# Graph layer 1 by lists: a 128-wide column selection, a DMA-shifted comparison, four sums in a bank, and half of the placings on ScalarE

## The chip, the cores and the metric

The kernel runs on one core of a Trainium2 chip. The metric is device time in microseconds; three runs of the kernel before gave 1370.18, 1371.73 and 1374.76, the median being 1371.73. The engines are TensorE (PE, with its weight loads PEld), VectorE (DVE), ScalarE (ACT), GpSimd (POOL) and SyncE (SP, which here only issues DMAs). A profile of one execution is read for where the time goes.

## The reference

Four graph layers act in turn on x (2708 x 128) with one sparse matrix adj (2708 x 2708). Each normalises its input, applies relu and adds its result to x. The change touches layer 1 only:

```python
s = node_feats @ msg_w[:, :D].T
d = node_feats @ msg_w[:, D:].T
messages = gelu(s[:, None, :] + d[None, :, :] + msg_b)
aggregated = einsum('ijd,ij->id', messages, adj)
combined = concatenate([node_feats, aggregated], axis=-1)
new_feats = combined @ upd_w.T + upd_b
h = gelu(new_feats) + node_feats            # then a layer norm over h
```

A message exists for every pair (i, j), but it counts only where adj[i, j] is not zero, which are few entries in a row. The diagonal is one of them.

## The kernel before

Rows are taken in 22 tiles (`NT`) of 128, columns in 22 blocks (`NB`) of 124 (`JB`). Layer 0 streams adj once, writes its transpose to memory on SP's queue, and keeps for every row and block the eight largest entries and their columns (`val`, `col`, `S` = 8), the diagonal (`own`) apart. If a row has more, or a tile more than 128 entries in a block, a dense version runs instead; it does not here.

Layer 1 packs the entries of one tile and one block into 128 slots (`E`), so that the gelu runs on slots and not on pairs. For tile t:

- `count_rows` counts the entries of each row and block; `rank` turns the counts into running sums by a matmul with a triangle of ones (`ends`: exclusive and inclusive sums).
- `describe` writes the values, split in three bf16 parts, the columns and the ranks into `xb`.
- `select_rows` makes the 0/1 matrix `sel` [row, slot, block] that says which row fills which slot: one comparison with the exclusive sums, one with the inclusive ones (`later`), and their difference, 128 x 2816 elements each.
- `fetch` multiplies each block's `sel` with `xb`, in two halves of 11 blocks; every slot then has its row's entries and rank (`y`, `lead`).
- `place` picks in each slot its own entry (`value`) and column (`where`), and makes two 0/1 matrices: `selT` [slot, column, block], the column selection, and `mine` [slot, row, block].
- `put_values` multiplies `mine` with `value` on GpSimd, in two halves of 11 blocks (`put`, the placings).
- `turn_columns` transposes `selT` block by block on TensorE, eight to a PSUM bank, and ScalarE copies them out as `cols`.
- `combine` adds, in PSUM, the row's part (`sel` against the three parts `s3` of s) and the column's part (`cols` against `d3`): six matmuls a block, four blocks to a bank. `activate` is the gelu on ScalarE. `gather` multiplies the gelus with `put` and sums all blocks of a tile in a bank, `agg`. `close_tile` adds the diagonal's term (`gs`, the gelu of the own row, times `dg`, a diagonal of `own`) and VectorE copies the sum to `aggT`.
- `sources` prepares s and the own row's gelu for two tiles; `update` does the second half of the layer for four tiles, in eight steps, two of which fall into most tiles.

The order of the work is written by hand in `period(t)` and kept as written on each engine; the semaphores are set from the buffers. A period has six stages k, each with four blocks (two in the last). While tile t is combined, tile t+1 is turned and placed, tile t+2 fetched and placed, tile t+3 ranked and selected. Pools set when a buffer is free: `once` has one buffer (`mine`, `later`, `picked`), `putpool` three halves of `put`, `selpool` four of `sel`, `acc` one bank for `agg`. Three periods run as a fill between the first steps of the layer; period 0 begins near 320 us, the last combine ends near 797 us.

Of the kernel before, what the change touches and what calls it, by code (L numbers as in the profile page):

```python
# [30 lines left out]
P = 128  # L31
# [29 lines left out]
def listed_layers(ctx: ExitStack, tc: tile.TileContext, x, adj, w, out, flag):  # L61
# [186 lines left out]
    with (  # L248
# [2 lines left out]
        tc.tile_pool(name="l1w", bufs=1) as once,  # L251
        tc.tile_pool(name="l1s", bufs=4) as selpool,
        tc.tile_pool(name="l1b", bufs=3) as three,
        tc.tile_pool(name="l1q", bufs=3) as putpool,
        tc.tile_pool(name="l1y", bufs=2, space=PSUM) as ypool,
        tc.tile_pool(name="l1m", bufs=2, space=PSUM) as mpool,
        tc.tile_pool(name="l1p", bufs=1, space=PSUM) as acc,
# [14 lines left out]
        nc.vector.tensor_copy(counts, count.unsqueeze(2).to_broadcast([P, P, NB]))  # L272
        part = fix.tile([P, 1], F32, name="part")
        nc.gpsimd.iota(part, [[0, 1]], base=0, channel_multiplier=1, allow_small_or_imprecise_dtypes=True)
        before = fix.tile([P, 2, P], BF16, name="before")
        nc.vector.tensor_scalar(before[:, 0, :], count, part, None, ALU.is_gt)
        nc.vector.tensor_scalar(before[:, 1, :], count, part, None, ALU.is_ge)
        ident_h = fix.tile([P, P], BF16, name="ident_h")
        nc.vector.tensor_copy(ident_h, ident)
        rows_n = fix.tile([P, NT, NB], BF16, name="rows_n")  # L280
        ends = fix.tile([P, NT, 2, NB], BF16, name="ends")
        d3 = fix.tile([P, NB, 3, D], BF16, name="d3")
        xb = [fix.tile([P, NB, C], BF16, name=f"xb{q}") for q in range(2)]
        for q in range(2):
# [10 lines left out]

        def count_rows(t):
            some = work.tile([P, NB, S], BF16, name="some")
            nc.gpsimd.tensor_scalar(some, val[:, t, :, :], 0.0, None, ALU.is_gt)
            with nc.allow_low_precision("counts up to 8"):
                nc.vector.reduce_sum(rows_n[:, t, :], some, AX.X)  # L300

        def rank(t):
            p = rpool.tile([P, CH], F32, tag="r", name="p_r")
            for q in range(2):
                nc.tensor.matmul(p[:, q * NB : (q + 1) * NB], before[:, q, :], rows_n[:, t, :], start=True, stop=True)
            nc.vector.tensor_copy(ends[:, t, :, :], p[:, 0 : 2 * NB].rearrange("p (q b) -> p q b", q=2))  # L306

        def describe(t):
            x = xb[t % 2]
            rest = work.tile([P, NB, S], F32, name="v_r")  # L310
            split([x[:, :, q * S : (q + 1) * S] for q in range(3)], val[:, t, :, :], rest)
            nc.gpsimd.tensor_copy(x[:, :, 3 * S : 4 * S], col[:, t, :, :])
            nc.gpsimd.tensor_copy(x[:, :, 4 * S], ends[:, t, 0, :])

        def select_rows(t):

            sel = selpool.tile([P, E, NB], BF16, name="sel")
            later = once.tile([P, E, NB], BF16, name="later")
            for q, dst in enumerate((sel, later)):
                nc.vector.tensor_tensor(  # L320
                    dst, counts, ends[:, t, q, :].unsqueeze(1).to_broadcast([P, E, NB]), ALU.is_ge
                )
            nc.vector.tensor_tensor(sel, sel, later, ALU.subtract)  # L323
            state[t] = dict(sel=sel, ys=[])

        def fetch(t, half):

# [12 lines left out]
        def place(t):  # L340

            st = state[t]
            lead = st["lead"]
            slot = work.tile([P, NB], F32, name="slot")
            nc.vector.tensor_scalar(slot, lead[:, 0, :], part, -1.0, ALU.subtract, ALU.mult)
            hot = work.tile([P, NB, S], F32, name="hot")
            nc.vector.tensor_tensor(
                hot,
                count[:, 0:S].unsqueeze(1).to_broadcast([P, NB, S]),
                slot.unsqueeze(2).to_broadcast([P, NB, S]),  # L350
                ALU.is_equal,
            )
            picked = once.tile([P, NB, 4, S], F32, name="picked")
            for half, y in enumerate(st.pop("ys")):
                bs = slice(half * HB, (half + 1) * HB)
                nc.vector.tensor_tensor(
                    picked[:, bs, :, :],
                    y[:, :, 0 : 4 * S].rearrange("p b (q s) -> p b q s", s=S),
                    hot[:, bs, :].unsqueeze(2).to_broadcast([P, HB, 4, S]),
                    ALU.mult,  # L360
                )
            value = work.tile([P, NB], F32, name="value")
            where = work.tile([P, NB], BF16, name="where")
            with nc.allow_low_precision("column numbers"):
                nc.vector.tensor_reduce(where, picked[:, :, 3, :], AX.X, ALU.max)
            selT = work.tile([P, JB, NB], BF16, name="selT")
            nc.vector.tensor_tensor(  # L367
                selT, counts[:, 0:JB, :], where.unsqueeze(1).to_broadcast([P, JB, NB]), ALU.is_equal
            )
            nc.vector.reduce_sum(value, picked[:, :, 0:3, :], AX.XY)  # L370
            mine = once.tile([P, P, NB], BF16, name="mine")
            nc.vector.tensor_tensor(  # L372
                mine, counts, lead[:, 1, :].unsqueeze(1).to_broadcast([P, P, NB]), ALU.is_equal
            )
            st["value"], st["selT"], st["mine"] = value, selT, mine

        def put_values(t, half):

            st = state[t]
            put = putpool.tile([P, HB, P], F32, name="put")  # L380
            bs = slice(half * HB, (half + 1) * HB)
            nc.gpsimd.tensor_tensor(  # L382
                put,
                st["mine"].rearrange("p i b -> p b i")[:, bs, :],
                st["value"][:, bs].unsqueeze(2).to_broadcast([P, HB, P]),
                ALU.mult,
            )
            st["put", half] = put

        def turn_columns(t, b0):  # L390

            st = state[t]
            if b0 == 0:
                st["cols"] = work.tile([P, NB, E], BF16, name="cols")
            n = min(8, NB - b0)
            p = ps.tile([P, 8, E], BF16, tag="ps", name="p_c")
            for b in range(n):
                nc.tensor.transpose(p[0:JB, b, :], st["selT"][:, :, b0 + b], ident_h)  # L398
            nc.scalar.copy(st["cols"][0:JB, b0 : b0 + n, :], p[0:JB, 0:n, :])  # L399

        own_rows = {}

        def sources(k):

# [22 lines left out]
            split([s3[:, q, :, :] for q in range(3)], sb[:, :, 0, :], rest)  # L427
            gs = three.tile([P, 2, D], F32, name="gs")
            nc.scalar.activation(gs, sb[:, :, 1, :], AF.Gelu)
            own_rows[k] = s3, gs  # L430

        def combine(t, k):
# [24 lines left out]
        def gather(t, k):  # L457

            st = state[t]
            m = size(t)  # L460
            if k == 0:
                st["agg"] = acc.tile([P, P], F32, name="agg1")
            g = st.pop(("g", k))
            for b in range(4 * k, min(4 * k + 4, NB)):
                put = st["put", b // HB][:, b % HB, 0:m]
                nc.tensor.matmul(st["agg"][:, 0:m], g[:, b - 4 * k, :], put, start=(b == 0), stop=False)  # L466

        aggs = {}

        def close_tile(t):  # L470

            st = state.pop(t)
            m = size(t)
            gs = own_rows[t // 2][1]
            if t // 4 not in aggs:
                aggs[t // 4] = work.tile([D, 4, P], F32, name="aggT")
            nc.tensor.matmul(st["agg"][:, 0:m], gs[0:m, t % 2, :], st["dg"][0:m, 0:m], start=False, stop=True)
            nc.vector.tensor_copy(aggs[t // 4][:, t % 4, 0:m], st["agg"][:, 0:m])


        STEPS = 8
# [51 lines left out]
        def period(t):  # L533

            now, c, b, a = (0 <= t + q < NT for q in range(4))
            last = 0 <= t - 1 < NT
            for k in range(GB):
                if now:
                    combine(t, k)
# [8 lines left out]
                    gather(t, k - 1)  # L548
                if k in (1, 2) and b:
                    fetch(t + 2, k - 1)  # L550
                if k == 1:
                    if c:
                        put_values(t + 1, 0)
                    if a:
                        describe(t + 3)
                if k == 2:
                    if now:
                        dg = work.tile([P, P], F32, name="dg1")
                        nc.scalar.activation(dg, ident, AF.Identity, scale=own[:, t : t + 1])
                        state[t]["dg"] = dg  # L560
                        if t % 2 == 0 and t + 2 < NT:
                            sources(t // 2 + 1)
                    if a:
                        select_rows(t + 3)
                    if now and t + 4 < NT:
                        count_rows(t + 4)
                    updates(t)
                    if c:
                        put_values(t + 1, 1)
                if k >= 3 and c:  # L570
                    turn_columns(t + 1, 8 * (k - 3))
                if k == 3 and b:
                    place(t + 2)


        def enter(g):
# [72 lines left out]
        nc.vector.reduce_sum(flag, lost[:, 0, :], AX.X)  # L649
        over = fix.tile([P, 2], F32, name="over1")  # L650
        many = once.tile([P, NT, NB], BF16, name="many")
        nc.vector.tensor_scalar(many, ends[:, :, 1, :], float(E), None, ALU.is_gt)
        nc.vector.reduce_sum(over[:, 0:1], many, AX.XY)
        nc.vector.tensor_scalar(many, val[:, :, :, S - 1], 0.0, None, ALU.is_gt)
        nc.vector.reduce_sum(over[:, 1:2], many, AX.XY)
# [708 lines left out]
```

## Time and profile before

| what | us |
|---|---|
| median of three runs | 1371.73 |
| the profiled execution | 1372.74 |
| its span | 1370.9 |
| layer 0, fill, loop of layer 1 (from the span's start, near) | 0 to 245, 245 to 320, 320 to 797 |
| layers 2 and 3 | from about 800 |
| mean granted TensorE clock (share of full) | 0.905 |

The profile lists busy time by engine, groups of instructions by line (count, busy time, mean of one, idle time of the engine before them and what ended it), a timeline, and the chain of work that ended last: each piece in it was released by the piece before. A matmul's time is from its start to its modelled end and overlaps the next one; in the chain only the part that counts is shown. A line such as `128*124 128x124` gives the weights' rows and columns and then the operand's shape.

### The profile page before, as it was taken

The page shows a single profiled execution, that of the slowest core. Times are in us where ns is not written, and L with a number is a line of the kernel's source. Part 1 is how long each engine was busy: PE and PEld are TensorE (multiplying, and loading weights), DVE is VectorE, ACT ScalarE, POOL GpSimd, SP SyncE. Part 2 cuts the span into 40 slices and gives each one's busy share as a digit, 9 for nine tenths or more (in the row PEclk, how much of TensorE's full clock was granted, in tenths as well). Part 3 has the DMA queues.
Part 4 walks back from the last instruction along what each step waited for, and adds up shares of the span by engine and source line. Part 5 has one row for each costly group of instructions (what it writes and reads, how often), then busy time and mean ns, then how long its engine had stood idle before and what let it go on. Part 6 is the DMA issues. An engine that isn't in the chain of part 4 may idle for free.

```text
span 1370.9 us, 22846 instructions
## 1 busy us (share of the span) xinstructions
PE 1177.2 (86%) x8590; PEld 945.0 (69%) x8590; DVE 968.1 (71%) x2971; ACT 602.4 (44%) x1188; POOL 374.9 (27%) x303
## 2 busy tenths in 40 slices
PE   4997878248999999999999968898967999999975
PEld 1554445247999999999999943333445898997763
DVE  5999999994677676877799237666554667666551
ACT  4865655134333333343343321222244666765633
POOL 2111120454566465555564320000000001001001
PEclk9999985557999999999999979999987998998985
DMA  9488854000000000000000044444210000000000
GB/s 364 160 305 289 278 200 163 16 0 1 1 1 2 1 1 1 2 1 1 1 2 1 2 141 162 162 163 143 86 29 1 1 1 9 9 1 10 7 1 13
DMA packets 47930, 93.72 MB, mean 68 GB/s; under 512 B 5654, under 2 KB 18022, under 8 KB 45102
## 3 DMA queue, kind: packets, MB, share of 16 engines
q1 hardware_dynamic: 41220, 89.40, 18.7%
q10 hardware_dynamic: 6590, 2.77, 0.8%
q8 instruction: 69, 1.13, 0.4%
q14 instruction: 51, 0.42, 0.1%
HBM read 61.44 MB, written 30.72 MB: 67 GB/s over the span
## 4 chain that ended last, share of the span: by engine, by line
PE 43%; DVE 41%; issue 7%; DMA 4%; POOL 2%; ACT 2%; ACTq 0%; POOLq 0%; DVEq 0%
PE att L853 11%; DVE col L215 9%; DVE val L214 6%; PE agg L466 6%; PE p_m L442 4%; PE p_c L398 4%; PE p_m L446 4%; PE p_agg L742 3%; DVE selT L367 2%; DVE later L320 2%; DVE mask L745 2%; PE y L334 2%; DMA a<-adjT 2%; PE p_o L888 2%; DVE sel L323 2%
## 5 line engine op out<-in xcount | busy, mean ns | idle before, releaser
L853 PE MATMUL att<-hv,wt 128*128 128x129 f32 (+3 forms) x1936 | 241.3, 282 | 5.7 <-DVE att L870 4.8
L853 PEld LDWEIGHTS att<-hv,wt 128*128 128x128 f32 (+3 forms) x1936 | 222.6, 191 | 22.5 <-issue 10.4
L847 DVE SCALAR_TENSOR_TENSOR wt<-e,mask 128x1024 f32<-128x1024 f32 (+2 forms) x132 | 144.8, 1098 | 68.0 <-PE att L853 64.0
L382 POOL TENSOR_TENSOR put<-mine,value 128x1408 f32<-128x1408 bf16 x44 | 156.7, 3562 | 115.0 <-DVE mine L372 64.9
L442 PE MATMUL p_m<-s,sel 128*128 128x128 bf16 x1452 | 179.2, 233 | 2.4 <-ACT s L289 1.2
L843 ACT ACTIVATE e<-row,minus_one,rho 128x1024 f32<-128x1024 f32 (+2 forms) x132 | 149.1, 1141 | 67.3 <-DVE wt L847 65.3
L446 PE MATMUL p_m<-d,cols 124*128 124x128 bf16 (+1 forms) x1452 | 163.6, 221 | 0.0
L118 POOL TENSOR_TENSOR n_r<-n_r,minus_half 128x4 f32<-128x4 f32 (+2 forms) x30 | 34.8, 1161 | 453.0 <-DVE n_r L117 441.2
L442 PEld LDWEIGHTS <-sel 128*128 128x128 bf16 x1452 | 149.9, 161 | 3.8 <-issue 2.9
L466 PE MATMUL agg<-put,g 128*128 128x128 f32 (+1 forms) x968 | 138.2, 284 | 14.6 <-DVE ends L306 12.3
L194 PE MATMUL acc<-a,hs 128*128 128x512 f32 (+2 forms) x264 | 122.3, 598 | 31.9 <-DMA a<-in_adj 21.9
L466 PEld LDWEIGHTS agg<-put,g 128*128 128x128 f32 x968 | 120.2, 194 | 16.3 <-issue 16.2
L398 PE MATMUL p_c<-ident_h,selT 128*124 128x128 bf16 x484 | 123.2, 396 | 1.1 <-ACT cols L399 1.1
L742 PE MATMUL p_agg<-a,hs 128*128 128x512 f32 (+2 forms) x264 | 117.7, 592 | 5.0 <-DMA a<-adjT 5.0
L398 PEld LDWEIGHTS <-selT 128*124 128x124 bf16 x484 | 121.2, 336 | 1.1 <-issue 1.1
L215 DVE FIND_INDEX8 col<-val,a 128x8 uint16<-128x124 f32 (+1 forms) x441 | 117.0, 274 | 0.0
L454 ACT ACTIVATE g<-p_m 128x512 f32<-128x512 f32 x132 | 74.0, 560 | 91.5 <-PE p_m L446 90.7
L399 ACT COPY cols<-p_c 124x1024 bf16<-124x1024 bf16 (+1 forms) x66 | 62.0, 941 | 116.2 <-PE p_c L398 116.2
L446 PEld LDWEIGHTS <-cols 124*128 124x128 bf16 (+1 forms) x1452 | 109.6, 102 | 0.6 <-issue 0.6
L194 PEld LDWEIGHTS acc<-a,hs 128*128 128x128 f32 (+1 forms) x264 | 49.1, 207 | 75.7 <-issue 42.4
L214 DVE MAX8 val<-a 128x8 f32<-128x124 f32 (+1 forms) x441 | 101.0, 264 | 0.0
L223 PEld LDWEIGHTS p_T<-ident,a 128*128 128x128 f32 x484 | 59.6, 147 | 54.9 <-ACT aT L227 25.9
(238 smaller groups left out, 1839.4 us busy)
## 6 DMA issues: line engine op xcount, KB each, us to landing
a<-in_adj SPq DMA_DIRECT2D x21, 1354.0 KB, 7.8
adjT<-aT SPq DMA_DIRECT2D x105, 256.0 KB, 2.6
a<-adjT SPq DMA_DIRECT2D x20, 1280.0 KB, 6.4
adjT<-aT SPq DMA_DIRECT2D x21, 74.0 KB, 2.7
a<-adjT SPq DMA_DIRECT2D x4, 370.0 KB
out<-xs SPq DMA_DIRECT2D x21, 64.0 KB, 1.5
xs<-in_x ACTq DMA_DIRECT2D x5, 256.0 KB
a<-adjT SPq DMA_DIRECT2D x5, 256.0 KB, 3.2
```

Of the source, the lines that this page charges most:

```text
L194: nc.tensor.matmul(accs[ci][:, 0:cw], h[0:m, n, :], a[0:m, c : c + cw], start=(n == 0), stop=(n == NT - 1))
L214: nc.vector.max(val[:, n, b, :], ab)
L215: nc.vector.max_index(col[:, n, b, :], val[:, n, b, :], ab)
L382: nc.gpsimd.tensor_tensor(put, st["mine"].rearrange("p i b -> p b i")[:, bs, :], st["value"][:, bs].unsqueeze(2).to_broadcast([P, HB, P]), ...
L398: nc.tensor.transpose(p[0:JB, b, :], st["selT"][:, :, b0 + b], ident_h)
L442: nc.tensor.matmul(p[:, b - b0, :], st["sel"][:, :, b], s3[:, q, t % 2, :], start=(q == 0), stop=False)
L446: nc.tensor.matmul(p[:, b - b0, :], st["cols"][0:kb, b, :], d3[0:kb, b, q, :], start=False, stop=(q == 2))
L466: nc.tensor.matmul(st["agg"][:, 0:m], g[:, b - 4 * k, :], put, start=(b == 0), stop=False)
L742: nc.tensor.matmul(pa[:, 0:n], h[0:k, j, :], a[0:k, j - j0, 0:n], start=(j == 0), stop=(j == NT - 1))
L843: nc.scalar.activation(e[0:kj, 0:n], row[0:kj, k, c : c + n], AF.Relu, bias=minus_one[0:kj, :], scale=rho[0:kj, j, k : k + 1])
L847: nc.vector.scalar_tensor_tensor(wt[0:kj, 0:n], e[0:kj, 0:n], 1.0, mask[0:kj, j, c : c + n], op0=ALU.add, op1=ALU.mult)
L853: nc.tensor.matmul(banks[s // 3][0:m, s % 3, :], wt[0:kj, q * P : q * P + m], hv[0:kj, j, k, :], start=(j == 0 and s % 3 == 0), stop=(j == ...
```

## The change

- `selT` has 128 columns instead of 124; the transposes and the copies to `cols` take all 128. `combine` still uses the width of the block.
- `rank` makes only the exclusive sums. `later` is no longer compared: a row's inclusive sum is the exclusive sum of the row after it, so SP copies `sel` from partitions 1 to 127 to partitions 0 to 126 of `later` by a DMA, and the subtraction moves into a new step `finish_rows`, at the end of stage 3, behind `place`. `later` has one buffer for the whole layer, set to zero once on GpSimd.
- `count_rows` runs on VectorE instead of GpSimd. The check at the end of the layer adds `rows_n` to `ends`.
- GpSimd makes the first half of `put` at the start of the period. The second half is made on ScalarE, one block at a time, two in a stage (`put_more`). `putpool` has four buffers.
- `agg` holds four tiles in one bank, and ScalarE copies it out once for the four, instead of VectorE once for each. `own` is multiplied into `gs` on ScalarE, and the diagonal's matmul uses the identity.

```diff
-        tc.tile_pool(name="l1q", bufs=3) as putpool,
+        tc.tile_pool(name="l1q", bufs=4) as putpool,
...
         def count_rows(t):
-            nc.gpsimd.tensor_scalar(some, val[:, t, :, :], 0.0, None, ALU.is_gt)
+            nc.vector.tensor_scalar(some, val[:, t, :, :], 0.0, None, ALU.is_gt)
...
         def rank(t):
-            for q in range(2):
-                nc.tensor.matmul(p[:, q * NB : (q + 1) * NB], before[:, q, :], rows_n[:, t, :], start=True, stop=True)
-            nc.vector.tensor_copy(ends[:, t, :, :], p[:, 0 : 2 * NB].rearrange("p (q b) -> p q b", q=2))
+            nc.tensor.matmul(p[:, 0:NB], before, rows_n[:, t, :], start=True, stop=True)
+            nc.vector.tensor_copy(ends[:, t, :], p[:, 0:NB])
...
         def select_rows(t):
             sel = selpool.tile([P, E, NB], BF16, name="sel")
-            later = once.tile([P, E, NB], BF16, name="later")
-            for q, dst in enumerate((sel, later)):
-                nc.vector.tensor_tensor(
-                    dst, counts, ends[:, t, q, :].unsqueeze(1).to_broadcast([P, E, NB]), ALU.is_ge
-                )
+            nc.vector.tensor_tensor(sel, counts, ends[:, t, :].unsqueeze(1).to_broadcast([P, E, NB]), ALU.is_ge)
+            nc.sync.dma_start(later[0 : P - 1, :, :], sel[1:P, :, :])
+            state[t] = dict(sel=sel, ys=[])
+
+        def finish_rows(t):
+            sel = state[t]["sel"]
             nc.vector.tensor_tensor(sel, sel, later, ALU.subtract)
-            state[t] = dict(sel=sel, ys=[])
...
-            selT = work.tile([P, JB, NB], BF16, name="selT")
-            nc.vector.tensor_tensor(
-                selT, counts[:, 0:JB, :], where.unsqueeze(1).to_broadcast([P, JB, NB]), ALU.is_equal
-            )
+            selT = work.tile([P, P, NB], BF16, name="selT")
+            nc.vector.tensor_tensor(selT, counts, where.unsqueeze(1).to_broadcast([P, P, NB]), ALU.is_equal)
...
-        def put_values(t, half):
+        def put_values(t):
+            for half in range(2):
+                st["put", half] = putpool.tile([P, HB, P], F32, name="put")
             nc.gpsimd.tensor_tensor(
-                put,
-                st["mine"].rearrange("p i b -> p b i")[:, bs, :],
-                st["value"][:, bs].unsqueeze(2).to_broadcast([P, HB, P]),
+                st["put", 0],
+                st["mine"].rearrange("p i b -> p b i")[:, 0:HB, :],
+                st["value"][:, 0:HB].unsqueeze(2).to_broadcast([P, HB, P]),
                 ALU.mult,
             )
+        def put_more(t, k):
+            st = state[t]
+            for b in range(HB + 2 * k, min(HB + 2 * k + 2, NB)):
+                nc.scalar.activation(
+                    st["put", 1][:, b - HB, :], st["mine"][:, :, b], AF.Identity, scale=st["value"][:, b : b + 1]
+                )
...
             for b in range(n):
-                nc.tensor.transpose(p[0:JB, b, :], st["selT"][:, :, b0 + b], ident_h)
-            nc.scalar.copy(st["cols"][0:JB, b0 : b0 + n, :], p[0:JB, 0:n, :])
+                nc.tensor.transpose(p[:, b, :], st["selT"][:, :, b0 + b], ident_h)
+            nc.scalar.copy(st["cols"][:, b0 : b0 + n, :], p[:, 0:n, :])
...
             nc.scalar.activation(gs, sb[:, :, 1, :], AF.Gelu)
+            for q in range(2):
+                t = 2 * k + q
+                nc.scalar.activation(gs[:, q, :], gs[:, q, :], AF.Identity, scale=own[:, t : t + 1])
...
         def gather(t, k):
-            if k == 0:
-                st["agg"] = acc.tile([P, P], F32, name="agg1")
+            if k == 0 and t % 4 == 0:
+                aggs[t // 4] = acc.tile([P, 4, P], F32, name="agg1")
+            agg = aggs[t // 4][:, t % 4, 0:m]
...
         def close_tile(t):
-            nc.tensor.matmul(st["agg"][:, 0:m], gs[0:m, t % 2, :], st["dg"][0:m, 0:m], start=False, stop=True)
-            nc.vector.tensor_copy(aggs[t // 4][:, t % 4, 0:m], st["agg"][:, 0:m])
+            nc.tensor.matmul(aggs[g][:, t % 4, 0:m], gs[0:m, t % 2, :], ident[0:m, 0:m], start=False, stop=True)
+            first, k = GROUPS[g]
+            if t == first + k - 1:
+                p = aggs[g]
+                aggs[g] = work.tile([D, 4, P], F32, name="aggT")
+                if m < P:
+                    nc.scalar.copy(aggs[g][:, 0 : k - 1, :], p[:, 0 : k - 1, :])
+                    nc.scalar.copy(aggs[g][:, k - 1, 0:m], p[:, k - 1, 0:m])
+                else:
+                    nc.scalar.copy(aggs[g][:, 0:k, :], p[:, 0:k, :])
...
         def period(t):
+            if c:
+                put_values(t + 1)
             for k in range(GB):
...
-                if k == 1:
-                    if c:
-                        put_values(t + 1, 0)
-                    if a:
-                        describe(t + 3)
+                if k == 1 and a:
+                    describe(t + 3)
                 if k == 2:
-                    if now:
-                        dg = work.tile([P, P], F32, name="dg1")
-                        nc.scalar.activation(dg, ident, AF.Identity, scale=own[:, t : t + 1])
-                        state[t]["dg"] = dg
-                        if t % 2 == 0 and t + 2 < NT:
-                            sources(t // 2 + 1)
+                    if now and t % 2 == 0 and t + 2 < NT:
+                        sources(t // 2 + 1)
...
-                    if c:
-                        put_values(t + 1, 1)
                 if k >= 3 and c:
                     turn_columns(t + 1, 8 * (k - 3))
+                if c:
+                    put_more(t + 1, k)
                 if k == 3 and b:
                     place(t + 2)
+                if k == 3 and a:
+                    finish_rows(t + 3)
```

More of the change, by code (lines that the diff above doesn't have):

```diff
@@ L274, in listed_layers @@
         nc.gpsimd.iota(part, [[0, 1]], base=0, channel_multiplier=1, allow_small_or_imprecise_dtypes=True)
-        before = fix.tile([P, 2, P], BF16, name="before")
-        nc.vector.tensor_scalar(before[:, 0, :], count, part, None, ALU.is_gt)
-        nc.vector.tensor_scalar(before[:, 1, :], count, part, None, ALU.is_ge)
+        before = fix.tile([P, P], BF16, name="before")
+        nc.vector.tensor_scalar(before, count, part, None, ALU.is_gt)
         ident_h = fix.tile([P, P], BF16, name="ident_h")
@@ L280, in listed_layers @@
         rows_n = fix.tile([P, NT, NB], BF16, name="rows_n")
-        ends = fix.tile([P, NT, 2, NB], BF16, name="ends")
+        ends = fix.tile([P, NT, NB], BF16, name="ends")
+        later = fix.tile([P, E, NB], BF16, name="later")
+        nc.gpsimd.memset(later, 0.0)
         d3 = fix.tile([P, NB, 3, D], BF16, name="d3")
@@ L312, in describe @@
             nc.gpsimd.tensor_copy(x[:, :, 3 * S : 4 * S], col[:, t, :, :])
-            nc.gpsimd.tensor_copy(x[:, :, 4 * S], ends[:, t, 0, :])
+            nc.gpsimd.tensor_copy(x[:, :, 4 * S], ends[:, t, :])
         def select_rows(t):
             sel = selpool.tile([P, E, NB], BF16, name="sel")
-            later = once.tile([P, E, NB], BF16, name="later")
-            for q, dst in enumerate((sel, later)):
-                nc.vector.tensor_tensor(
-                    dst, counts, ends[:, t, q, :].unsqueeze(1).to_broadcast([P, E, NB]), ALU.is_ge
-                )
+            nc.vector.tensor_tensor(sel, counts, ends[:, t, :].unsqueeze(1).to_broadcast([P, E, NB]), ALU.is_ge)
[3 more added lines that the diff above has]
+            sel = state[t]["sel"]
             nc.vector.tensor_tensor(sel, sel, later, ALU.subtract)
-            state[t] = dict(sel=sel, ys=[])
         def fetch(t, half):
@@ L375, in place @@
             st["value"], st["selT"], st["mine"] = value, selT, mine
-        def put_values(t, half):
+        def put_values(t):
             st = state[t]
-            put = putpool.tile([P, HB, P], F32, name="put")
-            bs = slice(half * HB, (half + 1) * HB)
+            for half in range(2):
+                st["put", half] = putpool.tile([P, HB, P], F32, name="put")
             nc.gpsimd.tensor_tensor(
-                put,
-                st["mine"].rearrange("p i b -> p b i")[:, bs, :],
-                st["value"][:, bs].unsqueeze(2).to_broadcast([P, HB, P]),
+                st["put", 0],
+                st["mine"].rearrange("p i b -> p b i")[:, 0:HB, :],
+                st["value"][:, 0:HB].unsqueeze(2).to_broadcast([P, HB, P]),
                 ALU.mult,
             )
-            st["put", half] = put
+        def put_more(t, k):
[4 more added lines that the diff above has]
+                )
         def turn_columns(t, b0):
@@ L397, in turn_columns @@
             for b in range(n):
-                nc.tensor.transpose(p[0:JB, b, :], st["selT"][:, :, b0 + b], ident_h)
-            nc.scalar.copy(st["cols"][0:JB, b0 : b0 + n, :], p[0:JB, 0:n, :])
-        own_rows = {}
+                nc.tensor.transpose(p[:, b, :], st["selT"][:, :, b0 + b], ident_h)
+            nc.scalar.copy(st["cols"][:, b0 : b0 + n, :], p[:, 0:n, :])
+        own_rows, aggs = {}, {}
         def sources(k):
@@ L465, in gather @@
                 put = st["put", b // HB][:, b % HB, 0:m]
-                nc.tensor.matmul(st["agg"][:, 0:m], g[:, b - 4 * k, :], put, start=(b == 0), stop=False)
-        aggs = {}
+                nc.tensor.matmul(agg, g[:, b - 4 * k, :], put, start=(b == 0), stop=False)
         def close_tile(t):
-            st = state.pop(t)
+            state.pop(t)
             m = size(t)
+            g = t // 4
             gs = own_rows[t // 2][1]
-            if t // 4 not in aggs:
-                aggs[t // 4] = work.tile([D, 4, P], F32, name="aggT")
-            nc.tensor.matmul(st["agg"][:, 0:m], gs[0:m, t % 2, :], st["dg"][0:m, 0:m], start=False, stop=True)
-            nc.vector.tensor_copy(aggs[t // 4][:, t % 4, 0:m], st["agg"][:, 0:m])
+            nc.tensor.matmul(aggs[g][:, t % 4, 0:m], gs[0:m, t % 2, :], ident[0:m, 0:m], start=False, stop=True)
[8 more added lines that the diff above has]
+                    nc.scalar.copy(aggs[g][:, 0:k, :], p[:, 0:k, :])
         STEPS = 8
@@ L651, in listed_layers @@
         many = once.tile([P, NT, NB], BF16, name="many")
-        nc.vector.tensor_scalar(many, ends[:, :, 1, :], float(E), None, ALU.is_gt)
+        nc.vector.tensor_tensor(many, ends, rows_n, ALU.add)
+        nc.vector.tensor_scalar(many, many, float(E), None, ALU.is_gt)
         nc.vector.reduce_sum(over[:, 0:1], many, AX.XY)
```

## The prediction

> **What bounds the kernel now.** I read the page's busy shares first, then the stretches between every second `sources` call (one even tile to the next, 18 tiles of layer 1 in all), then the chain of waits of one tile, then the costs by line, last the timeline of VectorE, GpSimd and ScalarE in one tile. The whole span does not decide; the pace of layer 1's loop does. Columns of the stretches: length, then busy time of PE, PEld, DVE, ACT, POOL, granted clock, DMA share, GB/s.
>
> ```profile
> PE 1177.2 (86%) x8590; PEld 945.0 (69%) x8590; DVE 968.1 (71%) x2971; ACT 602.4 (44%) x1188; POOL 374.9 (27%) x303
> ```
> ```profile
> 372.48:414.51 42.03, 41.54 (x454) 41.22 (x454) 30.75 (x32) 15.58 (x31) 24.23 (x13) 1.00 0.01 2
> ...
> 636.76:682.08 45.32, 42.73 (x453) 42.42 (x454) 35.44 (x57) 16.10 (x32) 25.21 (x15) 0.96 0.01 1
> ...
> sum 396.46, PE 384.17 PEld 381.05 DVE 300.41 ACT 148.76 POOL 228.09; mean PE 42.69 PEld 42.34 DVE 33.38 ACT 16.53 POOL 25.34
> ```
>
> 396.46 us for 18 tiles is 22.03 us a tile; PE is busy for 384.17/18 = 21.34 of it, DVE for 16.69, POOL for 12.67, ACT for 8.26. PE sets the pace; it idles 0.68 us a tile. What it spends, in the chain:
>
> ```profile
> 429.49 1.53 DVE mine L372
> 431.02 0.20 DVE aggT L478
> 431.22 0.12 DVE ends L306
> 431.34 0.02 issue
> 431.37 1.13 PE agg L466 x8
> 432.50 0.66 PE y L334 x11
> ...
> 440.61 1.87 PE p_c L398 x8
> ...
> 444.88 1.86 PE p_c L398 x8
> ...
> 448.43 1.39 PE p_c L398 x6
> ```
> ```profile
> L442 PEld LDWEIGHTS <-sel 128*128 128x128 bf16 x1056 | 109.0, 162 | 1.1 <-issue 0.4
> L398 PE MATMUL p_c<-ident_h,selT 128*124 128x128 bf16 x359 | 91.4, 396 | 0.0
> L398 PEld LDWEIGHTS <-selT 128*124 128x124 bf16 x360 | 90.2, 336 | 0.0
> L334 PEld LDWEIGHTS <-sel 128*128 128x128 bf16 x352 | 27.2, 166 | 0.0
> ```
>
> The reader should see two things. The 22 transposes of `selT` take 1.87 + 1.86 + 1.39 = 5.12 us, 233 ns each, while `fetch` (L334) loads 11 weights of the same layout, type and column step from `sel` in 0.66 us, 60 ns each: `sel` has 128 columns, `selT` 124, and the load lasts 336 ns against 162 to 166. And the idle time of PE ends in DVE: the first sum of a tile waits until `aggT` is copied out of the one bank, and that copy stands behind `mine`.
>
> Last, DVE and POOL hold each other up:
>
> ```profile
> 431.17 3.39 POOL L382 TENSOR_TENSOR put<-mine,value 128x1408 f32<-128x1408 bf16 x1 [5.68 <-DVE mine L372]
> 433.65 1.10 DVE L290 TENSOR_TENSOR v_r<-val,xb 128x176 f32<-128x176 f32 x1 [2.32 <-ACT xb L289]
> 440.54 3.35 POOL L382 TENSOR_TENSOR put<-mine,value 128x1408 f32<-128x1408 bf16 x1
> 441.39 2.53 DVE L345 TENSOR_SCALAR slot<-lead,part 128x22 f32<-128x22 bf16 x1
> ```
>
> `v_r`, 0.34 us when free, ends at 434.75, just after the put (434.56); `slot`, 0.25 when free, ends at 443.92, the put at 443.89.
>
> **The change, part by part, per tile.**
>
> *128 columns in selT.* The transposes keep count and moving side; only the weight's width changes. Ends: 60 ns each (fetch) and 233 (nothing gained). I take 65, as `p_m`'s same loads with 128 moving columns run at 0.19 to 0.21 us per three: 22 x (233 - 65) = 3.7 us off PE, all on the path. PE is then busy for 17.6. DVE writes 2816 instead of 2728 elements: 1.58 to 1.62 us. ScalarE's copies of `cols` keep their length (1.01, 1.01, 0.80).
>
> [...]
>
> *Four sums in one bank.* DVE loses `aggT` (0.28 us); ScalarE takes one 128x512 copy per four tiles (0.60 by L454's row, 0.15 a tile), in the queue after the first gelu of the tile; PE needs that bank again only after 1.47 us of `p_m`. The 0.68 us of PE idle ends here, unless another wait takes its place (next parts). `own` moves from ScalarE's `dg` (0.40 a tile) to two scalings of `gs` per two tiles (0.40 a tile): nothing.
>
> *Next-row comparison by DMA.* DVE loses `later` (2.03 us). SP gets one SBUF-to-SBUF DMA of 127 x 5632 bytes = 698 KB; the nearest rows land 256 KB in 2.6 to 3.2 us and 1280 KB in 6.4, so 4.4 us, ends 2.6 and 7.8 (1354 KB). SP's queue holds nothing else between the last `adjT` store and layer 2's loads, which come after layer 1. The subtraction (1.63) moves behind the eight instructions of `place`, 7.3 us by their rows (slot 0.25, hot 0.34, picked 0.96, where 0.34, selT 1.58, value 0.70, mine 1.62, gaps), so the DMA is covered at both ends. In the first fill tile nothing is placed, DVE waits bare: 4.4 + 0.3 - 1.95 = +2.7; the two other fill tiles lose `later` (1.95 and 4.72). I take 0 for the fill, ends -4 and +4.
>
> *Half of the placings on ScalarE.* POOL loses one put (3.36) and `some` (0.65 to 2.0); DVE gains `some` (0.2 to 0.35: the 484-element compare L654 takes 0.61) and loses waits behind the second put: mean minus free, slot 0.90 - 0.25 and selT 2.74 - 1.58, 1.8 us. ScalarE gains 11 activations of 128x128 with a scale per row and a source step of 22 elements. `dg` is that form with step 1: 0.40. No row shows ScalarE on the strided source; POOL reads it at 3363/1408 = 2.4 ns an element, which would make 0.21 + 0.31 = 0.52 us. Ends 0.35 (L289, 176 elements) and 1.0 (a 1024-element copy); I take 0.40, the same operation: 4.4 us. [...]
>
> *The new wait.* `mine` has one buffer. Its last reader is now ScalarE's 22nd placing, at the end of the tile, behind the last `cols` copy. So DVE waits there before it writes the next `mine`; behind `mine` stands the subtraction, and for that `fetch` on PE waits, 4.62 us into the next tile (two blocks of `p_m`, two of sums). From PE's last transpose: cols 0.80, placing 0.40, mine 1.62, subtraction 1.63, handovers 0.2 = 4.7 us. That is almost exactly 4.62: as it stands the loop costs PE 0.1 us a tile, and every lateness of ScalarE or DVE beyond it is PE's.
>
> ScalarE: 8.26 + 4.4 + 0.15 = 12.8 us of work, and in order it waits for the new `mine` (0.8), for fetch (0.9), and 2.3 us for `v_r`, which now stands behind the put that starts right after the subtraction: 17 us. DVE: 16.69 - 2.03 - 0.28 - 1.8 + 0.3 = 12.9, plus 3.2 behind that put and about 1 behind POOL's three copies for `xb`: 17 us. PE: 17.6. All three are nearly equal, and uneven over four tiles: walking the queues with these durations, the tile with `sources` and four scalings of `h` (ScalarE +1.9) comes to 20.4 us, that with `sources` and the moments of `xs` (DVE +2.7) to 20.3, the other two to 18.3 and 18.1: 19.3 in the mean. Late work is partly made up in the lighter tile after it, so I take 18.8, between this and 17.7.
>
> **Sum.** Periods 0 to 18: 19 x (22.03 - 18.8) = 61. Tiles 19 and 20 still turn columns but select nothing: 2 x 3.7 = 7. Tile 21 turns none. Fill 0. Together 68 us. The profiled execution took 1372.74 (span 1370.9 and 1.8 around it), 1 us above the median 1371.73. 1372.7 - 68 = 1304.
>
> **Rivals.**
> - *PE alone sets the pace* (17.7 us): 19 x 4.33 + 7 = 89, so 1283. For it: no single engine's sum exceeds PE's. Against: three queues in order with 17 us each.
> - *ScalarE and DVE run late*: placings of 0.52 add 1.3 us to ScalarE, or puts hit `sel` and `selT` as now (selT up to 4.49 in the trace): pace 20.5, 19 x 1.53 + 7 = 36, so 1337.
> - *The transposes stay at 233 ns*, because a transpose loads in its own way: PE stays at 21.34, the idle 0.68 goes, 0.1 comes: 19 x 0.6 = 11, so 1361. Against: the width of 336 to 166 ns in the same layout.
> - *Slower*: the strided source makes a placing expensive. ScalarE's tile is 12.8 - 4.4 + 4.2 of waits = 12.6 without placings; with the unevenness of 1.4 it reaches 22.03 at 0.73 us a placing. At the end of 1.0 it is 25 us: 19 x 3 + 2 x 1 = +59, so 1432. Against: `dg` at 0.40, and no ScalarE row of 128 elements over 0.49.
>
> **How the numbers follow.** Likeliest (18.1 to 19.7 us, 1287 to 1318): 0.50. PE alone: 0.20. Late: 0.20. Transposes unchanged: 0.04. Slower: 0.06. Range 1278 to 1338: PE alone with the fill 4 better, to the late case; outside lie the last two cases and the tail of the late one. A difference under 0.3% (4 us) could not be told from none. Faster 0.92, same 0.02, slower 0.06.
>
> **What would show it.** The load of `selT` at about 165 ns and 8 transposes in 0.5 us; no PE wait on `aggT`; instead `y` waiting for the subtraction, and `mine` waiting for ScalarE's placing; placings at 0.40; the DMA landing in 3 to 6 us with DVE waiting for it once; `v_r` stretched behind the put; pace near 18.8. Wrong if placings exceed 0.6 us, or if the transposes do not speed up.

## The result

The changed kernel takes 1725.37 us (four runs, 1722.9 to 1728.7) against 1371.99 for the kernel before: a ratio of 1.258, 95% interval 1.254 to 1.261. It is 353 us slower where 68 us faster was forecast, and it lies outside the range.

The page of the changed kernel, first line, and what stands at the top of its costliest groups:

```profile
PE 1132.5 (66%) x8568; PEld 892.1 (52%) x8568; DVE 872.5 (51%) x2949; ACT 703.1 (41%) x1437; POOL 234.7 (14%) x260
```
```profile
L335 PE MATMUL y<-xb,sel 128*128 128x34 bf16 x484 | 37.8, 221 | 346.2 <-DVE sel L325 346.2
L325 DVE TENSOR_TENSOR sel<-sel,later 128x2816 bf16<-128x2816 bf16 x22 | 35.8, 1626 | 416.5 <-DMA later<-sel 416.5
```

PE, DVE and POOL have less to do than before, ACT 100 us more, and none is the bound. DVE stands still for 416.5 us ahead of its 22 subtractions, always for the shift, and PE for 346.2 ahead of `fetch`, for the subtraction. The chain of the changed kernel over one round shows how (start, length, what):

```profile
587.37 29.38 DMA later<-sel
...
616.77 1.64 DVE sel L325
...
618.45 0.89 PE y L335 x11
...
623.82 0.97 PE p_s L419 x4
...
624.81 0.70 DVE sb L426
...
626.40 1.55 DVE sel L319
...
627.96 29.37 DMA later<-sel
```

The DMA, estimated at 4.4 us with an upper end of 7.8, takes 29.4. `place` and what else VectorE has to do cover a part of it only: 416.5/22 = 18.9 us a tile remain. So a closed loop decides: subtraction, first fetch, the next tile's `sel`, the next shift. In every second tile, as in the one shown, the second fetch, `sources` and the split of s lie in it too; from shift to shift it takes 40.6 us there and 34.4 in the others (553.00 to 587.37). PE's `sources` matmuls lie 75.0 us apart, for two tiles: a pace of 37.5 us against 22.03 before. From the first column matmul of `combine` to the last it is 762.3 us, before 474.9: 287 us more. The fill is 69 us longer (that first matmul starts at 390.0 instead of 321.2), because the three fill tiles wait for a shift each, at 257.38, 299.15 and 342.32 in the chain. What follows the loop is the same within 2 us. 287 + 69 - 2 = 354, against 354.7 between the two spans.

The stretch of that wait shows how little was moved (busy time of PE, PEld, DVE, ACT, POOL, then granted clock, share of the 16 DMA engines, GB/s):

```profile
587.37:616.74 29.37, 16.74 (x206) 16.53 (x204) 7.13 (x11) 9.87 (x19) 4.18 (x4) 0.85 0.06 25
```

The shift alone is 715 KB in 29.4 us, 24 GB/s. A share of 0.06 is about one sixteenth, as if one engine out of 16 moved it all. In the kernel before the page's first slice, with the 128-partition loads of layer 0, shows 364 GB/s.

### The profile page after: what moved, and what is told of

Read it like the earlier page. It is cut to its first block, busy times and chain, and to the rows that moved or that the text cites. A ratio compares the mean times of both kernels' runs of the same rounds, so it can differ in the third digit from the quotient of the medians.

```text
span 1725.6 us, 23023 instructions
## 1 busy us (share of the span) xinstructions
PE 1132.5 (66%) x8568; PEld 892.1 (52%) x8568; DVE 872.5 (51%) x2949; ACT 703.1 (41%) x1437; POOL 234.7 (14%) x260
## 4 chain that ended last, share of the span: by engine, by line
DMA 40%; PE 26%; DVE 25%; issue 5%; ACT 2%; POOL 2%; POOLq 0%; ACTq 0%; SPq 0%; DVEq 0%
DMA later<-sel 37%; PE att L866 9%; DVE col L215 7%; DVE val L214 5%; PE p_agg L755 3%; DVE sel L325 2%; DVE sel L319 2%; PE agg L476 2%; PE p_m L451 2%; PE y L335 1%; DMA a<-adjT 1%; PE p_m L455 1%; PE p_o L901 1%; PE p_o L900 1%; DVE mask L758 1%
## 5 line engine op out<-in xcount | busy, mean ns | idle before, releaser
L335 PE MATMUL y<-xb,sel 128*128 128x34 bf16 x484 | 37.8, 221 | 346.2 <-DVE sel L325 346.2
L325 DVE TENSOR_TENSOR sel<-sel,later 128x2816 bf16<-128x2816 bf16 x22 | 35.8, 1626 | 416.5 <-DMA later<-sel 416.5
L335 PEld LDWEIGHTS <-sel 128*128 128x128 bf16 x484 | 35.9, 166 | 349.9 <-DVE sel L325 349.8
L451 PE MATMUL p_m<-s,sel 128*128 128x128 bf16 x1452 | 190.4, 245 | 2.3 <-ACT s L290 1.2
L455 PE MATMUL p_m<-d,cols 124*128 124x128 bf16 (+1 forms) x1452 | 176.9, 235 | 0.0
L336 ACT CAST lead<-y 128x22 bf16<-128x22 f32 x44 | 7.9, 180 | 390.0 <-PE y L335 390.0
L451 PEld LDWEIGHTS <-sel 128*128 128x128 bf16 x1452 | 144.7, 156 | 4.0 <-issue 2.9
L392 ACT ACTIVATE put<-mine,value 128x128 f32<-128x128 bf16 x242 | 116.0, 525 | 18.0 <-DVE mine L371 18.0
L455 PEld LDWEIGHTS <-cols 124*128 124x128 bf16 (+1 forms) x1452 | 119.8, 110 | 0.6 <-issue 0.6
L381 POOL TENSOR_TENSOR put<-mine,value 128x1408 f32<-128x1408 bf16 x22 | 73.1, 3322 | 175.0 <-DVE mine L371 158.0
L223 PE MATMUL p_T<-ident,a 128*128 128x128 f32 x484 | 78.3, 296 | 18.2 <-DMA a<-in_adj 9.8
```

Source lines behind the costliest of these rows:

```text
L335: nc.tensor.matmul(y[:, b, :], st["sel"][:, :, bb], xb[t % 2][:, bb, :], start=True, stop=True)
L392: nc.scalar.activation(st["put", 1][:, b - HB, :], st["mine"][:, :, b], AF.Identity, scale=st["value"][:, b : b + 1])
L451: nc.tensor.matmul(p[:, b - b0, :], st["sel"][:, :, b], s3[:, q, t % 2, :], start=(q == 0), stop=False)
L455: nc.tensor.matmul(p[:, b - b0, :], st["cols"][0:kb, b, :], d3[0:kb, b, q, :], start=False, stop=(q == 2))
```

## The experiments

Theory A: the number of rows in a DMA sets how many of the 16 DMA engines share it. 127 is prime, so by this theory one engine moves everything. Theory B: this shift is slow in itself, by its size, its one-partition step, or its being inside the on-chip memory. Behind both stands a second question: whether the other parts of the change would have done what the forecast says. Each ratio is against runs of the kernel before on the same chip; the two versions with one run each have none.

### The shift in two pieces of 112 and 15 rows

```diff
-            nc.sync.dma_start(later[0 : P - 1, :, :], sel[1:P, :, :])
+            nc.sync.dma_start(later[0:112, :, :], sel[1:113, :, :])
+            nc.sync.dma_start(later[112:127, :, :], sel[113:128, :, :])
```

> The shift as two DMAs, partitions 1 to 112 and 113 to 127. Theory A (the number of rows of a DMA sets how many of the 16 DMA engines share it; 127 is prime, so one engine moves all 698 KB: 29.4 us at 24 GB/s, and a DMA share of 0.07 in the wait): 112 rows go to 16 engines with 7 each, 39 KB an engine at 24 GB/s = 1.6 us and some 2 us around it; DVE waits for the shift in the fill only, the pace of a tile is 18 to 19.5 us, the time 1285 to 1325. Theory B (a shift by one partition inside the on-chip memory, or 698 KB of it, is slow however it is cut): the larger piece still takes 112/127 of 29 us = 26 us, and the time stays above 1650.

1287.26 us, ratio 0.936 (0.931 to 0.940), so 88 us faster than the kernel before and 438 faster than the change as made. The same bytes, the same partition step, the same queue. The larger piece's landing, as the trace gives it for its line:

```profile
DMA to landing us min/median/max: 4.3/4.3/4.3
```

DVE waits for the shift in the fill alone (waits of VectorE from 250 to 330 us):

```profile
DVE sel L326 <- DMA later<-sel: 5.0, 1, 5.0
```

That wait lies in the first fill tile, where nothing covers the shift. Share of the 16 engines and GB/s in it (the last two columns), first in the change as made, then with 112 and 15 rows:

```profile
257.40:286.90 29.50, 0.00 (x0) 0.00 (x0) 0.00 (x0) 0.00 (x0) 0.74 (x3) 0.50 0.06 24
```
```profile
257.90:262.20 4.30, 0.00 (x0) 0.00 (x0) 0.00 (x0) 0.00 (x0) 0.44 (x2) 0.50 0.53 166
```

The same bytes now keep about half of the 16 engines busy. Theory B is out.

### 126 rows and 1 row

```diff
+            nc.sync.dma_start(later[0:126, :, :], sel[1:127, :, :])
+            nc.sync.dma_start(later[126:127, :, :], sel[127:128, :, :])
```

> The shift as 126 rows and 1 row. Theory A with any divisor (126 = 14 x 9, so 14 engines with 9 rows): 51 KB an engine at 24 GB/s = 2.1 us and some 2 around it, time within 10 us of the 112 and 15 version. Theory C (only whole multiples of 16 rows are shared): the 126 rows land after 29 us and the time is above 1700.

1287.28 us in the one run, the same as with 112 and 15. VectorE waits for the shift once, for 5.0 us, as with 112 and 15, and the share in that wait is 0.47. 126 is no multiple of 16, so theory C falls; theory A with any divisor (126 = 14 x 9) stands.

### 113 rows and 14 rows

```diff
+            nc.sync.dma_start(later[0:113, :, :], sel[1:114, :, :])
+            nc.sync.dma_start(later[113:127, :, :], sel[114:128, :, :])
```

> The shift as 113 rows and 14 rows: one row more in the large piece than the 112 of the version that ran at 1287 us. Theory A (the count's divisors set the engines; 113 is prime, 14 goes to 14 engines): one engine moves 113 rows in 29.4 x 113/127 = 26.2 us, the pace of a tile is 37.5 - 3.2 = 34.3 us, the time about 1725 - 22 x 3.2 = 1655. If the whole 127 was slow for any other reason (its size, the last partition), cutting it anywhere helps, and the time is near 1287.

1672.35 us in the one run. Two rounds of its chain:

```profile
498.24 25.98 DMA later<-sel
...
536.16 25.98 DMA later<-sel
```

One row more than 112 costs 385 us. The chain counts these 25.98 us from the issue of the second piece, which starts 0.7 us behind that of the first. Taken from the end of the first issue in both kernels, it is 26.0/113 = 0.23 us a row here and 28.8/127 = 0.23 in the change: the landing grows with the rows, at 24 GB/s in both. The whole time came out 17 us above the expectation. From the end of `sel` to the landing it is 26.7 us, not the expected 26.2, which makes 11 of the 17 over 22 tiles; the rest stays open.

Theory A agrees with all four counts: 113 and 127 rows moved at 24 GB/s, 112 and 126 landed within 5 us of the first issue. The share of the 16 engines was 0.06 with 127 rows in one piece, 0.53 with 112 and 15, 0.47 with 126 and 1; which engines took part, and what other counts do, was not shown.

### The change without its DMA

```diff
-            nc.sync.dma_start(later[0 : P - 1, :, :], sel[1:P, :, :])
+            nxt = work.tile([P, NB], BF16, name="nxt")
+            nc.vector.tensor_tensor(nxt, ends[:, t, :], rows_n[:, t, :], ALU.add)
+            nc.vector.tensor_tensor(later, counts, nxt.unsqueeze(1).to_broadcast([P, E, NB]), ALU.is_ge)
```

> The change without its DMA: the inclusive sums by one addition of 22 elements, later by a second comparison on VectorE behind the first, all other parts as changed. If the DMA alone broke the forecast, the walk of the forecast holds with 2.1 us more on VectorE: pace 19.3 to 20.9, time 1300 to 1345. If ScalarE's placings (0.52 us as measured, 11 a tile) or the wait of mine were a second cause, the pace stays above 22 and the time at 1370 or more.

1302.32 us, ratio 0.944 (0.938 to 0.950); the time is inside the expectation, the pace, 18.74 us (299.83 for 16 tiles), below its 19.3. So the other parts carry the gain. A shift that lands in time adds some 15 us to it: the ratio intervals of the two versions touch, but from the first column matmul to the last it is 406.0 us here and 391.4 with 112 and 15 rows. VectorE's work is 15.2 us a tile here and 13.4 there.

### The 128-wide selection alone

The kernel before, with `selT`, its transposes and the copies to `cols` as in the change and nothing else.

```diff
-            selT = work.tile([P, JB, NB], BF16, name="selT")
+            selT = work.tile([P, P, NB], BF16, name="selT")
...
-                nc.tensor.transpose(p[0:JB, b, :], st["selT"][:, :, b0 + b], ident_h)
+                nc.tensor.transpose(p[:, b, :], st["selT"][:, :, b0 + b], ident_h)
```

> The kernel before with the column selection 128 wide and nothing else. The transposes go from 233 to about 65 ns each, PE's work from 21.34 to 17.6 us a tile. VectorE has 16.7 us of work and waits for lead and v_r as before, and PE waits for aggT behind mine: pace 18.5 to 20.5, time 1295 to 1335. If the other parts of the change carry the gain, the pace stays at 21 or more and the time above 1350.

1363.09 us, ratio 0.990 (0.983 to 0.997): a miss. The transposes did become fast (a load of `selT` has a median of 156 ns), but most of the saving was lost. Waits of PE, first in the kernel before from 330 to 727 us, then here from 320 to 720 (total, times, longest):

```profile
PE agg L466 <- DVE ends L306: 12.3, 10, 2.6
```
```profile
PE agg L466 <- DVE ends L306: 53.0, 12, 6.2
```

PE, quicker, arrives at the first sum of a tile while VectorE is still busy with `place`; `aggT` stands behind it. The wait carries the name of `ends`, the instruction behind `aggT` on VectorE. The pace is 389.94/18 = 21.66 us. PE idles for 3.0 of it, 2.3 more than before. Its work is 335.85/18 = 18.66 us a tile and not 17.6: the mean granted clock over these 18 tiles is 0.92, where it was 0.99 before. So of the 3.7 us some 2.3 went into the wait and 1 into slower work, and 0.4 was left.

### Four sums in a bank, alone and with the selection

```diff
-            if k == 0:
-                st["agg"] = acc.tile([P, P], F32, name="agg1")
+            if k == 0 and t % 4 == 0:
+                aggs[t // 4] = acc.tile([P, 4, P], F32, name="agg1")
...
-            nc.vector.tensor_copy(aggs[t // 4][:, t % 4, 0:m], st["agg"][:, 0:m])
+            if t == first + k - 1:
+                p = aggs[g]
+                aggs[g] = work.tile([D, 4, P], F32, name="aggT")
+                ...
+                    nc.scalar.copy(aggs[g][:, 0:k, :], p[:, 0:k, :])
```

On the kernel before, this part alone:

> The kernel before with four sums in a bank and nothing else. PE's 0.68 us of idle time a tile, which ends in the copy of aggT, goes: 19 x 0.68 = 13 us, so 1355 to 1364. If that wait is replaced by another (puts, fetch), nothing is gained: 1368 and more.

1345.11 us, ratio 0.981 (0.978 to 0.985), twice the gain that the idle time promised and below the expected 1355 to 1364. 14 tiles of it:

```profile
329.90:624.53 294.63, 294.63 (x3215) 293.45 (x3214) 232.53 (x258) 115.86 (x234) 178.57 (x98) 1.00 0.01 2
```

PE is busy all the time, 21.04 us a tile. It was 21.34 before, where the granted clock stood at 0.96 in two of the nine stretches; set against the same stretches of this run, those two hold somewhat over half of the difference, and the rest lies in stretches at 1.00. Together 0.99 us a tile, or 19 us over the loop's 19 full periods; the loop from first to last is 20.8 shorter, and the layers after it took 7 us less in that profile, which nothing in the edit explains.

With the selection:

> The kernel before with two parts of the change: the 128-wide selection and four sums in a bank, copied out by ScalarE once for four (the diagonal's matmul as before). With the selection alone the pace is 21.7 us, PE has 18.7 of work and waits 3 us a tile, mostly for aggT behind mine on VectorE. Theory D (that copy's place in VectorE's queue is the bound): the pace falls to 18.3 to 19.7, time 1295 to 1325. Theory E (VectorE and GpSimd, with 16.5 and 12.7 us of work and each other's locks, are the bound themselves): the wait moves to a put or a fetch, pace over 20.5, time over 1340.

1313.96 us, ratio 0.958 (0.955 to 0.961): theory D. The two parts alone give 1 and 2%, together 4%: from the first column matmul to the last they save 12.3 and 20.8 us alone and 54.2 together. The pace is 19.45 us, and DVE is busy for 283.03/16 = 17.7 of it. Two of its comparisons are stretched (VectorE's groups, busy time and mean in ns):

```profile
L320 DVE TENSOR_TENSOR sel<-counts,ends 128x2816 bf16<-128x2816 bf16 x16 | 53.4, 3335 | 0.0
L367 DVE TENSOR_TENSOR selT<-counts,where 128x2816 bf16<-128x2816 bf16 x16 | 43.7, 2730 | 0.6
```

Both take 1.62 us when free. GpSimd works beside the long ones: a `sel` of 4.76 us starts at 457.53, and GpSimd makes a put and three copies for `xb` from 457.39 to 466.0 without a break.

### The second half of the placings back on GpSimd

In the version with 112 and 15 rows, `put_more` makes the half in one GpSimd instruction, in the third stage.

```diff
-            for b in range(HB + 2 * k, min(HB + 2 * k + 2, NB)):
-                nc.scalar.activation(
-                    st["put", 1][:, b - HB, :], st["mine"][:, :, b], AF.Identity, scale=st["value"][:, b : b + 1]
-                )
+            if k == 2:
+                nc.gpsimd.tensor_tensor(
+                    st["put", 1],
+                    st["mine"].rearrange("p i b -> p b i")[:, HB:NB, :],
+                    st["value"][:, HB:NB].unsqueeze(2).to_broadcast([P, NB - HB, P]),
+                    ALU.mult,
+                )
```

> The changed kernel with the shift in 112 and 15 rows, and the second half of the placings back on GpSimd, at the third stage. Theory: PE sets the pace at 17.6 us of work; VectorE has 13.4 us plus 1.8 of waits behind the second put, ScalarE loses 5.7 us; pace 17.9 to 19, time 1283 to 1310. Rival (ScalarE's half is what lets VectorE keep up): a pace over 20, time over 1325.

1309.53 us, ratio 0.956 (0.952 to 0.959). The time is at the end of the expectation, the pace (268.34/14 = 19.17) just above it. ScalarE's half is worth 22 us by the medians, 27 by the ratios, which are from different chips. PE now waits longer for the subtraction; from 320 to 720 us, first with ScalarE's half, then here:

```profile
PE y L336 <- DVE sel L326: 1.9, 7, 0.5
```
```profile
PE y L336 <- DVE sel L326: 24.7, 13, 3.7
```

### The new wait of mine

Two ways to take it away from the version with 112 and 15 rows. First, a second buffer, paid for by `aggT`, `v_r` and `hot` with one each:

```diff
-            mine = once.tile([P, P, NB], BF16, name="mine")
+            mine = work.tile([P, P, NB], BF16, name="mine")
```

> The shift in 112 and 15 rows, and two buffers for mine (to make room, aggT, v_r and hot get one instead of two). With one buffer the pace was 17.96 us, PE's work 17.61. Theory (the forecast's new wait, mine behind ScalarE's last placing and fetch behind the subtraction, costs PE what is left of the difference): pace 17.7 to 17.9, time 1279 to 1287. Rival (the single buffers that made room cost more, or the wait was hidden): 1287 or more.

1282.71 us, ratio 0.932 (0.927 to 0.936), pace 17.80, both inside the expectation. Second, one buffer, but the subtraction ahead of `mine`:

```diff
-        def place(t):
+        def place(t, then):
...
+            if then is not None:
+                finish_rows(then)
             mine = once.tile([P, P, NB], BF16, name="mine")
...
-                    place(t + 2)
-                if k == 3 and a:
+                    place(t + 2, t + 3 if a else None)
+                if k == 3 and a and not b:
                     finish_rows(t + 3)
```

> The shift in 112 and 15 rows, one buffer for mine, but the subtraction stands ahead of mine on VectorE, so that fetch no longer waits for ScalarE's last placing. The shift then has the 5.6 us from sel to value as cover, for a landing of 4.3. Same theory: pace 17.7 to 17.9, time 1279 to 1287. Rival: the shift is not landed in time or mine now comes late for the placings, 1287 or more.

1277.94 us, ratio 0.929 (0.924 to 0.933), pace 284.34/16 = 17.77. The time is just below the expected 1279 to 1287. It is the fastest of the case, 7% under the kernel before. PE's work is 17.48 us a tile there, so little is left of waits; what PE still waits for from 320 to 640 us is the gelu on ScalarE, 5.3 us in six waits. The shift is less covered in this order, and VectorE waits for it again, 1.9 us in three waits. The intervals of this run, of the two buffers and of the version with neither overlap: that the wait cost something is likely (all three paces fall in that order, 17.96, 17.80, 17.77), its size is a few microseconds. `count_rows` on VectorE and `own` in `gs` were not tried by themselves.

## Why the prediction was wrong

**The step that failed** is the price of the shift: "the nearest rows land 256 KB in 2.6 to 3.2 us and 1280 KB in 6.4, so 4.4 us, ends 2.6 and 7.8" and "so the DMA is covered at both ends". It measured 29.4. The rows were near in size but all moved 128 partitions; 127 is another case, and the bound was laid along the bytes when the count of rows decided. With 112 and 15 rows the landing of the larger piece is 4.3 us and all but the first shift is covered, so the price was right for another shape. The cover was weak as well: the upper end of 7.8 us lay above the 7.3 named for it, and the rows listed for the 7.3 add up to 5.8 without gaps. No rival held a late shift: at 29.4 the loop through the subtraction, `fetch` and the next `sel` decides.

**The fill.** Taken as 0 within 4; it was +69, three bare shifts instead of one of 4.4. With the shift in two pieces it is -0.5 (first matmul at 320.7).

**The transposes.** Right. The weight load of the changed kernel:

```profile
L404 PEld LDWEIGHTS <-selT 128*128 128x128 bf16 x286 | 23.9, 153 | 0.0
```

153 ns instead of 336, and in the chain of the version with 112 and 15 rows:

```profile
493.37 0.53 PE p_c L405 x8
...
496.32 0.52 PE p_c L405 x8
...
498.53 0.39 PE p_c L405 x6
```

1.44 us a tile for 5.12, 65 ns each as taken: 3.7 us saved. The load became 2.2 times as fast, the pace 3.6 times.

**PE's floor.** 17.6 us was forecast. The version with 112 and 15 rows, 16 tiles:

```profile
sum 287.30, PE 281.80 PEld 276.67 DVE 214.57 ACT 198.31 POOL 119.78; mean PE 35.22 PEld 34.58 DVE 26.82 ACT 24.79 POOL 14.97
```

281.80/16 = 17.61. DVE 13.4 (forecast 12.9), ACT 12.4 (12.8).

**The pace without the slow DMA.** Forecast 18.8, measured 17.96. The walk through the queues gave 19.3, with each tile keeping its whole lateness; that the lighter tiles make up nearly all of it is the likely reason it was too high, which no run shows by itself. The rival "PE alone sets the pace", at 17.7 and 1283, is what the shift in two pieces shows (1287). The two waits of the walk are there, with little effect on PE: `v_r` behind the put has a median of 1.99 us, and `mine` waits 31.1 us for ScalarE from 320 to 640, while PE waits 1.7 for the subtraction.

**The placings.** 0.52 us each in the profile against 0.40 taken; 0.52 is the number that the prediction had worked out from GpSimd's strided reads and set aside. Two in a row take 0.85 to 0.97 together. The rival *ScalarE and DVE run late* made a pace of 20.5 of placings of 0.52; the placings came so, and with the shift in two pieces the pace was 17.96. The rival that made them expensive enough to slow the kernel needed 0.73.

**Four sums in a bank.** Forecast as the end of 0.68 us of idle time a tile. Alone it gave twice that, and its 14 tiles show a clock of 1.00 throughout; without it the fast transposes are worth 1%, which the prediction, costing the two apart, did not say.

## What to carry to other kernels

Before a DMA's price is read from a row, compare the count of its outermost dimension with that of the row, not only the bytes: 112 or 126 rows of 5.6 KB were hidden, 113 and 127 took 0.23 us a row. In place of the one DMA of 127 rows, two of 112 and 15 or of 126 and 1 cost one more issue, 0.5 to 0.8 us on SP, and the kernel took 438 us less. When a saving on the busiest engine is forecast, ask first which copy it will next wait for: here 3.7 us a tile on PE were worth 1% alone; together with four tiles in the one bank that VectorE emptied late, which alone gave 2%, they were worth 4%.

## What the runs showed that was not expected

Short waits of PE went with a lower granted clock. With none it was 1.00 and PE's work 21.04 us a tile; with 0.68 us of idle time a tile it dipped to 0.96 in stretches, and the work was 21.34. With the 128-wide selection alone, at 3.0 us of idle time, it was 0.92, and the work 18.66 us; with four sums in a bank added to it the idle time was 1.3 us, the clock 0.97 and the work 18.16. That the waits caused the dips was not tried by itself.

The issue of a small DMA took long in one version: SP needed 8.8 us for that of the 14 rows behind 113 rows, but 0.8 us for 15 rows behind 112 and 0.5 us for 1 row behind 126. Why was not tried.
